# Layer 1's support stage in a hand-written order with four product banks, its first transposes placed at the end of layer 0

## The chip, the cores and the metric

The kernel runs on one core of a Trainium2 chip. The metric is the device time of one execution in microseconds (us), here the median of a few runs. The engines are named as in the profile: PE (TensorE matmul), PEld (its weight loads), DVE (VectorE), ACT (ScalarE), POOL (GpSimd) and SP (SyncE, which here only issues DMAs). SBUF is the on-chip working memory, PSUM the buffer with eight banks into which PE writes.

## The reference

Four graph layers follow each other on x (4096 × 256, float32) with one 0/1 adjacency matrix adj (4096 × 4096). Each layer ends in a layernorm of x plus the layer's result.

```python
# layer 0: attention over the adjacency, 8 heads of 32
x = layernorm(x + L0(x, W, b, a, adj))
# layer 1: the layer of this change
support = x @ weight                      # 4096 x 256
A = jnp.diagonal(adj) + adj               # the diagonal is added to every row
x = layernorm(x + (A @ support + bias))
# layer 2: two steps of top-p attention and of diffusion over adj + I
x = layernorm(x + L2(x, adj, W1, W2, W3, U1, U2, ln_g, ln_b))
# layer 3: mean over neighbours, one product, relu
x = layernorm(x + L3(x, adj, W, b))
```

Since the diagonal is added to every row, A @ support is adj @ support plus one row, diagonal @ support, which is the same for all rows of the result.

## The kernel before

Rows are tiled in NB = 32 blocks of 128. X, the running x, stays in SBUF for all 32 blocks.

**Layer 0** goes through its heads in two halves, and in each through four stretches of eight row blocks. A head accumulates into a PSUM tile `acc` of four banks; two buffers of it take all eight banks. After a head DVE reduces acc (L334) and a chain of short DVE steps follows (L338 to L345). In the second half the two halves of the columns are added to X (L359 on POOL, L360 on POOL or, for the last eight blocks, on DVE), two blocks at a time. Each such pair of blocks goes into the list `later`; its layernorm is done on POOL while a later head runs. Four pairs, the blocks 24 to 31, are left over and handed to layer 1 as `self.later`.

**Layer 1, the support stage** (`layer1`) first prepares two small weight products for layer 2 (`attention_weights`: two transposes L758, two copies L759, matmuls L762, and copies into `wkq` L763 and L764). Their inputs lie in the tile `xT1[1]` until they are used. Then it goes through eight groups of four row blocks. For a group, `transposed` (L99 to L110) makes eight 128 × 128 transposes on PE into two `ps_tp` banks (L108) and ACT copies them (L109) into one of the two tiles `xT1`. In groups 1 to 4 the layernorm of one left-over pair runs: `moments` takes statistics on DVE (L85, L86), POOL works out the inverse deviation (L88, L89), and DVE normalizes (L96). Then each of the four blocks is multiplied by the weight into a `ps_sup` bank (L781), and `split` writes the product in two parts into XD: the rounded value by ACT (L126) and the remainder by DVE (L127). There are two `ps_sup` banks, two `ps_tp` and two `ps_adj`. After the groups, 32 matmuls with the diagonal (L786) give the common row.

**Layer 1, the product.** For each of the 32 row blocks b, four pieces of the adjacency (128 × 8 × 128) are cast from bytes `na` into `adj_piece`, on DVE for even and on ACT for odd pieces (L206, L204). There are eight piece buffers, two blocks' worth. 32 matmuls (L802) multiply them by XD into `ps_adj`. `keep` writes every piece out to `adjs` in DRAM for the later layers, on SP's queue (L161, L165, L168), with the identity added to the block on the diagonal by POOL (L164). The bytes come in by ACT's DMA queue, four loads of 1 MB for eight row blocks (`bytes_of`, L189), in eight buffers. A block ends with three additions to X, a layernorm and a store (L807 to L811).

**What sets the order.** Nothing in this stretch is ordered by hand. A scheduler lists the instructions of every engine by its own estimates, so work of the product (casts, write-outs, ps_adj matmuls) is mixed into the support stage. The order is fixed once compiled, and each engine goes through its list in that order. Inside `tc.manual_schedule(...)` the named engines follow the order of the program text; layers 2 and 3 use it in places already.

Of the kernel before, what the change touches and what calls it, by code (L numbers as in the profile page):

```python
# [9 lines left out]
F32 = mybir.dt.float32  # L10
I32 = mybir.dt.int32
F32R = mybir.dt.float32r
BF16 = mybir.dt.bfloat16
FP8 = mybir.dt.float8e4
# [5 lines left out]
ET = mybir.EngineType  # L20
# [3 lines left out]
P = 128  # L24
# [31 lines left out]
class Net:  # L56
# [135 lines left out]

    def adj_pieces(self, pool, nas, b, G=8):

        nc = self.nc
        at = b * P % self.IT
        if at == 0:
            nas[:] = self.bytes_of(pool, b)
        pieces = []
        for g in range(self.NB // G):  # L200
            a = pool.tile([P, G, P], F32R, name="adj_piece", bufs=2 * (self.NB // G))
            edges = nas[g][:, :, at:at + P].bitcast(FP8)
            if g % 2:
                nc.scalar.mul(a, edges, 2.0 ** 5)  # L204
            else:
                nc.vector.tensor_scalar_mul(a, edges, 2.0 ** 5)  # L206
            pieces.append(a)
        return pieces

# [3 lines left out]
    def layer0(self):  # L215
        nc, tc, NB, D, N = self.nc, self.tc, self.NB, self.D, self.N
# [3 lines left out]
        Q = IT // P  # L220
        keep = self.ctx.enter_context(tc.tile_pool(name="l0k", bufs=1, space=DRAM))
        self.fits = keep.tile([1, 1], I32, name="fits")
        with ExitStack() as ctx:
            pool = ctx.enter_context(tc.tile_pool(name="l0", bufs=1))
# [58 lines left out]
            X, xr = self.X, self.rows(self.x)  # L283
            gp = ctx.enter_context(tc.tile_pool(name="l0gm", bufs=1))
            work = ctx.enter_context(tc.tile_pool(name="l0w", bufs=2))
            psum = ctx.enter_context(tc.tile_pool(name="l0ps", bufs=2, space=PSUM))
# [6 lines left out]
            for half in range(2):  # L293
                for it in range(N // IT):
# [14 lines left out]
                    for hh in range(H // 2):  # L309
# [4 lines left out]
                        acc = psum.tile([P, Q, 256], F32, name="acc")  # L314
                        for g in range(NB // K):
# [8 lines left out]
                            for k in range(K):  # L324
                                jc = g * K + k
                                for q in range(Q):
# [3 lines left out]
                                                     start=(jc == 0 and q % 2 == 0),  # L330
                                                     stop=(jc == NB - 1 and q % 2 == 1))
# [25 lines left out]
                    for q in range(0, Q, 2):  # L357
# [2 lines left out]
                        engine.tensor_add(xs[:, :, D // 2:], xs[:, :, D // 2:], y[:, q:q + 2])  # L360
                        later.append(xs)
            self.later = later

    def choose0(self, fac, zd, gmd, gm0):

        with self.tc.If(self.nc.values_load(self.fits, min_val=0, max_val=1) == 0):  # L366
            self.general0(fac, zd, gmd, gm0)
# [384 lines left out]
    def attention_weights(self, psum):  # L752

        nc, A = self.nc, 64
        aw1, aw3, aw2, w1 = self.attention_parts()
        for c in range(2):
            pt = psum.tile([P, 512], F32, name="ps_sup")
            nc.tensor.transpose(pt[:A, :P], aw1[:, c, :], self.ident)  # L758
            nc.scalar.copy(w1[:, c, :], pt[:A, :P])  # L759
        for c in range(2):  # L760
            pt = psum.tile([P, 512], F32, name="ps_sup")
            nc.tensor.matmul(pt[:, :A], w1[:, c, :], aw2, start=True, stop=True)  # L762
            nc.vector.tensor_copy(self.wkq[:, c, 1, :], pt[:, :A])  # L763
            nc.vector.tensor_copy(self.wkq[:, c, 0, :], aw3[:, c, :])  # L764

    def layer1(self):
        nc, tc, NB, D, X = self.nc, self.tc, self.NB, self.D, self.X
        with self.ctx1 as ctx:
            pool, w1, bias, dg = self.pool1, self.weight1, self.bias1, self.diagr
            work = ctx.enter_context(tc.tile_pool(name="l1w", bufs=2))  # L770
            psum = ctx.enter_context(tc.tile_pool(name="l1ps", bufs=2, space=PSUM))
            XD = self.XD
            self.attention_weights(psum)
            for g in range(NB // 4):
                xT = self.transposed(psum, work, X[:, 4 * g:4 * g + 4, :], "xT", out=self.xT1[g % 2])
                if 1 <= g <= 4:
                    self.layernorm(work, self.later[g - 1], self.later[g - 1])
                for q in range(4):
                    ps = psum.tile([P, 512], F32, name="ps_sup")
                    for c in range(2):  # L780
                        nc.tensor.matmul(ps[:, :D], xT[:, c, q * P:(q + 1) * P], w1[:, c, :],  # L781
                                         start=(c == 0), stop=(c == 1))
                    self.split(XD[:, 4 * g + q], ps[:, :D])
            pd = psum.tile([P, 512], F32, name="ps_sup")
            for jc in range(NB):
                nc.tensor.matmul(pd, dg[:, jc:jc + 1].to_broadcast([P, P]), XD[:, jc].rearrange("p s d -> p (s d)"),  # L786
                                 start=(jc == 0), stop=(jc == NB - 1))
            row = pool.tile([P, D], F32, name="row1")
            nc.vector.tensor_add(row, pd[:, :D], bias)
            nc.vector.tensor_add(row, row, pd[:, D:])  # L790

            nas = []
            ahead = self.adj_pieces(work, nas, 0)
            for b in range(NB):
                ps = psum.tile([P, 512], F32, name="ps_adj")
                now, ahead = ahead, None
                for g, a in enumerate(now):

                    self.keep(work, a, b, g)
                    for k in range(8):  # L800
                        jc = g * 8 + k
                        nc.tensor.matmul(ps, a[:, k, :], XD[:, jc].rearrange("p s d -> p (s d)"),  # L802
                                         start=(jc == 0), stop=(jc == NB - 1))
                if b + 1 < NB:
                    ahead = self.adj_pieces(work, nas, b + 1)
                xb = X[:, b:b + 1, :]
                nc.vector.tensor_add(xb[:, 0], xb[:, 0], ps[:, :D])  # L807
                nc.vector.tensor_add(xb[:, 0], xb[:, 0], ps[:, D:])
                nc.vector.tensor_add(xb[:, 0], xb[:, 0], row)
                self.layernorm(pool, xb, xb)  # L810
                nc.gpsimd.dma_start(self.xd[b, :, 0, :], xb[:, 0])  # L811
# [1158 lines left out]
```

## Time and profile before

| | |
|---|---|
| median of 3 runs | 4007.29 us (4001.58 to 4010.75) |
| the profiled execution | 4011.93 us, of which the span is 4010.2 us |
| PE busy in the span | 3906.8 us (97%) |
| DVE, ACT, POOL busy | 2990.2, 2742.6, 1136.7 us (75%, 68%, 28%) |
| last matmul of layer 0 ends | 1322.3 us |
| support stage, with the diagonal | 1324.2 to 1395.9 us |
| last matmul of layer 1's product starts | 1623.4 us |

Times inside the span count from its start. The profile is of one execution, and a matmul's end in it is modelled: the pitch from one start to the next says more than a busy time. A row of the timeline gives start, time, engine, source line, operation, output and inputs and a count of merged instructions; in brackets stands the idle time of that engine before it and who ended it. A line such as L96 is in a helper and has several callers.

### The profile page before, as it was taken

Reading aid. Unit: us, or ns where it says so; the run is one execution under the profiler, and the core shown is the slowest. Engines: PE = TensorE matmul, PEld = TensorE weight load, DVE = VectorE, ACT = ScalarE, POOL = GpSimd, SP = SyncE. Lnnn points to the kernel's source line nnn. Section 1 sums busy time; section 2 is a strip of 40 time slices with the busy share of each in tenths; the row PEclk is TensorE's granted clock in tenths of the full one; section 3 lists DMA queues with packets and bytes.
Section 4 is the critical chain, followed back from the end, with each engine's and each line's share of the span. In section 5 each row is a group of like instructions: output and inputs, shape, how many; then the busy total and the mean of one; then the engine's idle time right before and its main releaser. Section 6 shows DMA issues by size and latency. Waiting matters only on the chain. (4 is left out here: it accounts for less than half of the span.)

```text
span 4010.2 us, 68765 instructions
## 1 busy us (share of the span) xinstructions
PE 3906.8 (97%) x25081; PEld 3377.3 (84%) x25081; DVE 2990.2 (75%) x6647; ACT 2742.6 (68%) x5119; POOL 1136.7 (28%) x1394
## 2 busy tenths in 40 slices
PE   8899998999999899999999999999999999999899
PEld 7899998999999788678888888865888888888687
DVE  7742228999999444567878788837999999999365
ACT  5532228999999322468888888825888888888132
POOL 1321111111344022411111111114555555555211
PEclk9999999999999999999999999999999999999999
DMA  4765557335222498533333333463333333335541
GB/s 130 228 204 176 176 168 224 90 108 136 69 78 70 170 359 324 154 119 96 100 97 101 95 102 92 137 203 105 108 107 104 108 118 99 107 120 184 186 158 49
DMA packets 317403, 557.36 MB, mean 139 GB/s; under 512 B 72646, under 2 KB 139734, under 8 KB 312950
## 3 DMA queue, kind: packets, MB, share of 16 engines
q1 hardware_dynamic: 242368, 396.99, 31.4%
q0 software_dynamic: 32224, 98.75, 7.5%
q10 hardware_dynamic: 42454, 57.04, 4.3%
q8 instruction: 203, 3.33, 0.3%
q14 instruction: 154, 1.26, 0.1%
HBM read 386.71 MB, written 165.94 MB: 138 GB/s over the span
## 5 line engine op out<-in xcount | busy, mean ns | idle before, releaser
L1359 PE MATMUL ps_a<-X,aT 128*128 128x256 f32 x4096 | 970.4, 379 | 1.3 <-ACT h L1500 1.1
L1359 PEld LDWEIGHTS ps_a<-X,aT 128*128 128x128 f32 x4096 | 774.1, 190 | 127.2 <-issue 3.3
L328 PE MATMUL acc<-gm,gt 128*128 128x198 bf16 x8192 | 702.5, 248 | 14.2 <-DVEq L366 5.6
L328 PEld LDWEIGHTS <-gt 128*128 128x128 fp8e4 x8192 | 700.4, 97 | 16.2 <-issue 11.3
L273 ACT ACTIVATE sg<-lpb,nlc 128x1024 fp8e4<-128x1024 f32 x632 | 664.0, 1135 | 48.5 <-DVE gt L275 33.8
L550 PE MATMUL pz<-src,ar 128*128 128x264 f32 x4096 | 513.5, 288 | 20.6 <-DVE ar L540 18.6
L550 PEld LDWEIGHTS pz<-src,ar 128*128 128x128 f32 x4096 | 510.3, 191 | 23.7 <-DVE ar L540 21.3
L180 PE MATMUL ps_r<-XD,adj_piece 128*128 128x512 f32 x1888 | 528.4, 414 | 1.0 <-DMA adj_piece<-adjs 1.0
L1086 ACT ACTIVATE ja<-e,nc 128x2048 uint8<-128x2048 f32 x240 | 480.9, 2004 | 2.0
L1352 ACT COPY aT<-ps_tp 128x512 f32<-128x512 f32 x512 | 296.4, 579 | 216.7 <-PE ps_tp L1350 214.5
L180 PEld LDWEIGHTS ps_r<-XD,adj_piece 128*128 128x128 f32 x1888 | 332.9, 189 | 70.2 <-issue 12.9
L1151 DVE MAX8 cand<-v 128x8 f32<-128x256 f32 x1024 | 347.1, 411 | 4.4
L1201 DVE SCALAR_TENSOR_TENSOR e<-e,edge 128x512 f32<-128x512 f32 x512 | 347.9, 751 | 2.1
L543 ACT ACTIVATE nb<-ar 128x512 uint8<-128x512 f32 x256 | 147.5, 623 | 268.4 <-DVE ar L540 265.2
L1350 PE MATMUL ps_tp<-ident,e 128*128 128x128 f32 x2048 | 307.7, 273 | 0.0
L1147 DVE SCALAR_TENSOR_TENSOR v<-e,hi 128x2048 f32<-128x2048 f32 x128 | 299.8, 2342 | 2.4
L1350 PEld LDWEIGHTS ps_tp<-ident,e 128*128 128x128 f32 x2048 | 256.5, 141 | 51.4 <-issue 0.5
L267 DVE TENSOR_SCALAR sg<-lpb,nlc 128x1024 fp8e4<-128x1024 f32 x384 | 285.2, 778 | 6.6 <-SPq L366 4.4
L995 ACT ACTIVATE e<-ps_logit 128x1024 f32<-128x1024 f32 x256 | 260.2, 1027 | 26.6 <-PE ps_logit L993 26.4
L993 PE MATMUL ps_logit<-kT,q 128*128 128x512 f32 x1024 | 274.1, 409 | 4.0 <-ACT e L995 1.7
L540 DVE CAST ar<-a 128x1024 fp32r<-128x1024 f32 x128 | 88.9, 695 | 248.1 <-PE pz L550 242.4
L802 PE MATMUL ps_adj<-XD,adj_piece 128*128 128x512 f32 x1024 | 244.9, 398 | 1.2 <-POOL ln_var L88 1.2
(396 smaller groups left out, 5577.5 us busy)
## 6 DMA issues: line engine op xcount, KB each, us to landing
adj_piece<-adjs SPq DMA_DIRECT2D x552, 256.0 KB, 2.9
a<-in_adjt_dram SPq DMA_DIRECT2D x256, 256.0 KB, 3.0
adjs<-adj_piece SPq DMA_DIRECT2D x96, 512.0 KB, 3.4
na<-nad SPq DMA_DIRECT2D x64, 512.0 KB, 4.5
lpb<-lpd POOLq DMA_DIRECT2D x32, 512.0 KB, 4.2
nad<-nb POOLq DMA_DIRECT2D x128, 128.0 KB, 2.8
na<-nad ACTq DMA_DIRECT2D x16, 1024.0 KB, 5.6
gmd<-gb POOLq DMA_DIRECT2D x64, 198.0 KB, 3.9
```

The source lines that it names most:

```text
L180: nc.tensor.matmul(ps, a[:, k, :], rhs(jc).rearrange("p s d -> p (s d)"), start=(jc == 0), stop=(jc == self.NB - 1))
L267: nc.vector.tensor_scalar(sg[:, k, :], lpb, nlc[:, 4 * g + k, h:h + 1], 2.0 ** -5, op0=ALU.is_ge, op1=ALU.mult, saturate=False)
L273: nc.scalar.activation(sg[:, k, :], lpb, AF.Sign, scale=-1.0, bias=nlc[:, 4 * g + k, h:h + 1], saturate=False)
L328: nc.tensor.matmul(acc[:, q, :6 * C1], gt[:, k, q * P:(q + 1) * P], gm0[:, jc, :] if head0 else gm[:, jc, hh, :], start=(jc == 0 and q % 2 ...
L550: nc.tensor.matmul(pz[q][:, t, :W], ar[:, q, k, :], src[:, jc, t, s], start=(jc == 0 and s == 0), stop=(jc == NB - 1 and s == 1))
L1086: nc.scalar.activation(ja, e[:, s * HALF:(s + 1) * HALF], f, bias=nc1, accum_out=fs[:, i + s:i + s + 1])
L1147: nc.vector.scalar_tensor_tensor(v, ec, hi, ec, op0=ALU.is_lt, op1=ALU.mult, accum_out=sb[:, s:s + 1])
L1151: nc.vector.max(cand[:, 8 * j:8 * j + 8], v[:, k * 256:(k + 1) * 256])
L1201: nc.vector.scalar_tensor_tensor(ec, ec, edge[:, j:j + 1], ec, op0=ALU.is_ge, op1=ALU.mult)
L1350: nc.tensor.transpose(pt[:, k * P:(k + 1) * P], e[:, jc * P:(jc + 1) * P], self.ident)
L1352: nc.scalar.copy(aT, pt)
L1359: nc.tensor.matmul(pa[:, :D], aT[:, k * P:(k + 1) * P], X[:, jc, :], start=(jc == 0), stop=(jc == NB - 1))
```

## The change

- The whole support stage stands in a manual schedule for PE, ACT, DVE, POOL and SP.
- `ps_sup` has four banks instead of two, so that the stage's pool takes all eight banks.
- The transposes of group 0 move to the end of layer 0, into a buffer of `acc`; ACT copies them to `xT1[0]`. Those of group g + 1 stand between the second and the third product tile of group g.
- `attention_weights` becomes a generator: its transposes come first, its matmuls and copies after the second product tile.
- The four left-over layernorms normalize on POOL instead of DVE, after the tiles of groups 0 to 3.
- The first four loads of bytes are issued after group 1. The four pieces of block 0 are cast one each after groups 4 to 7. To this end `adj_pieces` is split, and `adj_part` casts a single piece.

```diff
--- before.py
+++ after.py
@@ -192,20 +192,21 @@
 
     def adj_pieces(self, pool, nas, b, G=8):
 
+        if b * P % self.IT == 0:
+            nas[:] = self.bytes_of(pool, b)
+        return [self.adj_part(pool, nas, b, g) for g in range(self.NB // G)]
+
+    def adj_part(self, pool, nas, b, g, G=8):
+
         nc = self.nc
         at = b * P % self.IT
-        if at == 0:
-            nas[:] = self.bytes_of(pool, b)
-        pieces = []
-        for g in range(self.NB // G):
-            a = pool.tile([P, G, P], F32R, name="adj_piece", bufs=2 * (self.NB // G))
-            edges = nas[g][:, :, at:at + P].bitcast(FP8)
-            if g % 2:
-                nc.scalar.mul(a, edges, 2.0 ** 5)
-            else:
-                nc.vector.tensor_scalar_mul(a, edges, 2.0 ** 5)
-            pieces.append(a)
-        return pieces
+        a = pool.tile([P, G, P], F32R, name="adj_piece", bufs=2 * (self.NB // G))
+        edges = nas[g][:, :, at:at + P].bitcast(FP8)
+        if g % 2:
+            nc.scalar.mul(a, edges, 2.0 ** 5)
+        else:
+            nc.vector.tensor_scalar_mul(a, edges, 2.0 ** 5)
+        return a
 
 
 
@@ -360,6 +361,12 @@
                         engine.tensor_add(xs[:, :, D // 2:], xs[:, :, D // 2:], y[:, q:q + 2])
                         later.append(xs)
             self.later = later
+            acc = psum.tile([P, Q, 256], F32, name="acc").rearrange("p q c -> p (q c)")
+            for c in range(2):
+                half = acc[:, c * 512:(c + 1) * 512]
+                for q in range(4):
+                    nc.tensor.transpose(half[:, q * P:(q + 1) * P], X[:, q, c * P:(c + 1) * P], self.ident)
+                nc.scalar.copy(self.xT1[0][:, c, :], half)
 
     def choose0(self, fac, zd, gmd, gm0):
 
@@ -754,11 +761,12 @@
         nc, A = self.nc, 64
         aw1, aw3, aw2, w1 = self.attention_parts()
         for c in range(2):
-            pt = psum.tile([P, 512], F32, name="ps_sup")
+            pt = psum.tile([P, 512], F32, name="ps_sup", bufs=4)
             nc.tensor.transpose(pt[:A, :P], aw1[:, c, :], self.ident)
             nc.scalar.copy(w1[:, c, :], pt[:A, :P])
+        yield
         for c in range(2):
-            pt = psum.tile([P, 512], F32, name="ps_sup")
+            pt = psum.tile([P, 512], F32, name="ps_sup", bufs=4)
             nc.tensor.matmul(pt[:, :A], w1[:, c, :], aw2, start=True, stop=True)
             nc.vector.tensor_copy(self.wkq[:, c, 1, :], pt[:, :A])
             nc.vector.tensor_copy(self.wkq[:, c, 0, :], aw3[:, c, :])
@@ -770,18 +778,31 @@
             work = ctx.enter_context(tc.tile_pool(name="l1w", bufs=2))
             psum = ctx.enter_context(tc.tile_pool(name="l1ps", bufs=2, space=PSUM))
             XD = self.XD
-            self.attention_weights(psum)
-            for g in range(NB // 4):
-                xT = self.transposed(psum, work, X[:, 4 * g:4 * g + 4, :], "xT", out=self.xT1[g % 2])
-                if 1 <= g <= 4:
-                    self.layernorm(work, self.later[g - 1], self.later[g - 1])
-                for q in range(4):
-                    ps = psum.tile([P, 512], F32, name="ps_sup")
-                    for c in range(2):
-                        nc.tensor.matmul(ps[:, :D], xT[:, c, q * P:(q + 1) * P], w1[:, c, :],
-                                         start=(c == 0), stop=(c == 1))
-                    self.split(XD[:, 4 * g + q], ps[:, :D])
-            pd = psum.tile([P, 512], F32, name="ps_sup")
+            nas, ahead = [], []
+            with tc.manual_schedule(engines={ET.PE, ET.Activation, ET.DVE, ET.Pool, ET.SP}):
+                setup = self.attention_weights(psum)
+                next(setup)
+                for g in range(NB // 4):
+                    xT = self.xT1[g % 2]
+                    for q in range(4):
+                        ps = psum.tile([P, 512], F32, name="ps_sup", bufs=4)
+                        for c in range(2):
+                            nc.tensor.matmul(ps[:, :D], xT[:, c, q * P:(q + 1) * P], w1[:, c, :],
+                                             start=(c == 0), stop=(c == 1))
+                        self.split(XD[:, 4 * g + q], ps[:, :D])
+                        if q == 1:
+                            if g == 0:
+                                for _ in setup:
+                                    pass
+                            if g < NB // 4 - 1:
+                                self.transposed(psum, work, X[:, 4 * g + 4:4 * g + 8, :], "xT", out=self.xT1[(g + 1) % 2])
+                    if g < 4:
+                        self.layernorm(work, self.later[g], self.later[g], nc.gpsimd)
+                        if g == 1:
+                            nas[:] = self.bytes_of(work, 0)
+                    else:
+                        ahead.append(self.adj_part(work, nas, 0, g - 4))
+            pd = psum.tile([P, 512], F32, name="ps_sup", bufs=4)
             for jc in range(NB):
                 nc.tensor.matmul(pd, dg[:, jc:jc + 1].to_broadcast([P, P]), XD[:, jc].rearrange("p s d -> p (s d)"),
                                  start=(jc == 0), stop=(jc == NB - 1))
@@ -789,8 +810,6 @@
             nc.vector.tensor_add(row, pd[:, :D], bias)
             nc.vector.tensor_add(row, row, pd[:, D:])
 
-            nas = []
-            ahead = self.adj_pieces(work, nas, 0)
             for b in range(NB):
                 ps = psum.tile([P, 512], F32, name="ps_adj")
                 now, ahead = ahead, None
```

## The prediction

> **What bounds the kernel now.** I read the page first: TensorE (PE) is busy 97% of the span, so a change pays only where PE idles or runs slowly. I compared the compiled instruction order of the two kernels next: apart from line and tile numbers, they differ on every engine only from the end of layer 0's last head to the first blocks of layer 1's product. So I cut that stretch into windows (columns: us, then busy time with instruction count of PE, PEld, DVE, ACT, POOL; granted clock; DMA share; GB/s).
>
> ```profile
> 1322.00:1396.00 74.00, 62.88 (x283) 50.88 (x282) 29.38 (x77) 25.85 (x56) 6.26 (x12) 0.91 0.59 206
> 1322.00:1332.00 10.00, 8.08 (x32) 6.29 (x31) 6.73 (x17) 2.34 (x6) 0.00 (x0) 0.66 0.00 1
> ...
> 1366.00:1373.00 7.00, 6.07 (x16) 4.90 (x17) 1.78 (x4) 2.14 (x6) 0.00 (x0) 0.51 1.02 364
> ...
> 1410.00:1500.00 90.00, 90.00 (x388) 72.11 (x387) 42.98 (x96) 25.43 (x24) 22.74 (x50) 1.00 0.93 361
> ```
>
> From 1322 to 1396 PE idles 74.00 − 62.88 = 11.1 us, and for about 7 us twice it runs at half clock. From 1410 on it never idles at full clock: the product is bound by PE, so whatever the stage before it saves reaches the end of layer 1. Next PE's own timeline:
>
> ```profile
> 1324.22 0.41 PE L758 MATMUL ps_sup<-ident,xT 128*64 128x128 f32 x2 [1.90 <-DVE red L334]
> ...
> 1337.32 1.96 PE L781 MATMUL ps_sup<-w,xT 128*128 128x256 f32 x8 [3.15 <-DVE XD L127]
> ...
> 1346.56 1.89 PE L781 MATMUL ps_sup<-w,xT 128*128 128x256 f32 x8
> 1348.29 1.04 PE L108 MATMUL ps_tp<-ident,X 128*128 128x128 f32 x8
> 1349.08 0.71 PE L802 MATMUL ps_adj<-XD,adj_piece 128*128 128x512 f32 x2
> ...
> 1366.93 2.07 PE L781 MATMUL ps_sup<-w,xT 128*128 128x256 f32 x4 [4.00 <-DVE XD L127]
> ...
> 1388.41 7.67 PE L786 MATMUL ps_sup<-XD,diagr 128*128 128x512 f32 x32
> 1395.92 4.36 PE L802 MATMUL ps_adj<-XD,adj_piece 128*128 128x512 f32 x18
> ```
>
> Who made PE wait 3.15 and 4.00 us is seen on DVE and ACT:
>
> ```profile
> 1336.43 0.41 DVE L96 TENSOR_SCALAR X<-X,ln_mv,ln_rstd 128x256 f32<-128x256 f32 x1 [0.83 <-POOL ln_rstd L89]
> 1336.76 0.75 DVE L127 TENSOR_TENSOR XD<-ps_sup,XD 128x256 fp32r<-128x256 f32 x2
> ...
> 1365.10 1.06 ACT L204 ACTIVATE adj_piece<-na 128x1024 fp32r<-128x1024 fp8e4 x1 [5.51 <-DMA adjs<-adj_piece]
> ...
> 1366.06 0.63 ACT L126 CAST XD<-ps_sup 128x256 fp32r<-128x256 f32 x2
> ```
>
> Both are queueing, not work. The subtractions that free the two ps_sup banks stand behind layernorm steps that wait for POOL; later the copies out of ps_sup stand behind a cast of an adjacency piece for a later block, which waits until its buffer has been written out.
>
> **What the Trainium skill says.** "TensorE: Matmul & The Clock Gate", section "What's actually happening": the clock halves after an idle window of about 3.4 us and returns after a busy one. The trace agrees: 0.50 from 1325 to 1332 after a gap of 1.9 us and thin work, and 0.51 from 1366 to 1373 after the gap of 4.0; each lasts about two such windows. "PSUM — Partial Sum Buffer", section "Engine vs sequencer instructions": ScalarE's, VectorE's and GpSimd's queues are strict FIFO; the fence above shows it. "SBUF — State Buffer", section "Who interferes with whom": a DVE instruction with two SBUF inputs, or in a two-port mode, blocks a GpSimd instruction that reads SBUF; one with at most one SBUF input does not. The trace has both prices for POOL's layernorm step, with DVE nearly full of mask work (X) and elsewhere (h):
>
> ```profile
> L96 POOL TENSOR_SCALAR h<-h,ln_mv,ln_rstd x64: 1239/1244/1248, 2828.0 to 3779.4; 128x256 f32<-128x256 f32 x64
> L96 POOL TENSOR_SCALAR X<-X,ln_mv,ln_rstd x24: 1217/2286/3707, 1074.4 to 1279.7; 128x256 f32<-128x256 f32 x24
> ```
>
> **The change part by part.** First the work that PE cannot avoid before 1395.92, in steady rates: two product tiles take 1348.29 − 1346.56 = 1.73 us, so 32 take 27.7; eight transposes 0.79, so eight groups 6.3; diagonal 7.5; attention weights about 1.0; a ps_adj matmul 0.2335 (blocks of 16 follow each other at 3.74 us), and 48 of them stand before 1395.92: 11.2. Sum 53.7, against 1395.92 − 1322.32 (the last head's end) = 73.6. So 19.9 us are to be had: 11.1 idle, up to 6.8 of half clock (0.34 of 10 us, 0.49 of 7), the rest pacing by two banks (two tiles per 2.06 us around 1381).
>
> *Start.* Eight transposes go into the free acc buffer while DVE reduces the last head; the first half's ACT copy (0.59) stands before the second half's transposes, so with about 0.2 per handover xT1[0] is ready near 1324.8. The weights' transposes wait for that and for the reduction (1324.17): PE starts its first two tiles near 1325.0, against 1327.2 before. Weights and transposes for group 1 follow to 1328.1, tiles 2 and 3 to 1329.8. Group 1's xT overwrites xT1[1], which holds the attention weights, so its ACT copies wait for the four wkq copies on DVE. Those stand behind the end of the last head, the four additions L360 (1.43), and two subtractions: near 1329.65. Two copies later group 1 can run; its tiles count from about 1330.4.
>
> *Groups 1 to 7.* Four banks allow 4 × 0.865 = 3.46 us from one use of a bank to its next; the round trip of a bank (matmul 0.87, ACT 0.37, DVE 0.42, handovers) was 2.06. So PE sets the pace: 3.46 + 0.79 = 4.25 per group. ACT needs 4 × 0.37 + 2 × 0.54 = 2.6, DVE 4 × 0.42 plus about 1.1 for the statistics = 2.8: both are hidden. Seven groups, less the last one's transposes, plus six ps_adj matmuls that stay inside (1.4): 29.8 − 0.8 + 1.4, ending near 1360.8.
>
> *Moved: na loads.* Four issues of 1 MB stand together on ACT after group 1. A similar four elsewhere, on SP:
>
> ```profile
> 3791.72 2.13 SPq L1844 DMA_DIRECT2D X<-nad  x4
> ```
>
> 2.1 us on ACT delays group 2's copies and, through its second xT, PE by about 0.5; bounds 0 and 2. The first load starts at about 1337 instead of 1331.25, and with 5.6 us to landing is there by 1343; its cast on DVE comes after group 4, near 1348.5. The second four are single issues, 0.33 each, hidden in ACT's slack. SP's write-outs start at 1349 instead of 1341, its own-block part behind POOL's last layernorm. Nothing reads these bytes in layer 1; they only free the eight piece buffers, first needed again after 1369.
>
> *Moved: layernorms to POOL.* Eight DVE steps of 0.41 vanish; POOL gets per group 0.23 + 0.72 + 2 × 1.24 plus gaps = 3.6 us. The DVE work beside it reads PSUM and at most one SBUF operand, so I take 1.24; the dear end is 2.3 to 3.7. At 3.6 they end by about 1350; the last rows are transposed near 1354.
>
> *Sum.* 1360.8 + 0.5 = 1361.3; diagonal 7.5: 1368.8. The 42 ps_adj matmuls no longer done by then: 9.8. That is 1378.6 against 1395.9: 17.3 us less. If the clock still halves at the start (gaps of about 1.5 us remain there), the first tiles to 1332 cost 3 us more. I take 16.3, one third of that. The profiled execution is 4011.93, of which the span is 4010.2: it would come to 3995.6. The median of the runs is 4007.29, 4.6 below it: 3991.0.
>
> **The rivals.**
> *DMA becomes the bound.* By the windows some 88 MB move between 1330 and 1624. In the shorter stage they would have from 1337 to 1607, 327 GB/s. Against it: from 1400 to 1600 the same mix already moved 343 GB/s on average, with PE never idle. For it: the share touches 1.03. If writes hold PE up at the end, most of the gain goes: 4004, within 0.2%.
> *Partial.* POOL's four layernorms run at the 7.8 us of layer 0's tail (four of them from 1251.3 to 1282.3). Started at 1333.3, they end at 1364.5 where 1354 is needed: 10.5 lost, 4001; a halved clock and a longer issue on ACT alone give 3995.
> *Slower.* The same place at its worst: the longest of those four took 1263.96 to 1275.71, 11.7 us. Four such end at 1380.1. The last transposes, and DVE's aggregates that need a free ln_mv buffer, wait 26 us: 17 saved, 26 lost, 4016. It decides from (1371.3 − 1333.3)/4 = 9.5 us each. Against it speaks what DVE runs here.
> *The change doesn't do what it says.* The compiled order excludes this: four banks, and only six ps_adj matmuls in the stage.
>
> **How the numbers follow.** About 0.2% (8 us) is what a measurement of this kernel can tell from no change; three runs of before spread over 9. Main case (13 to 18 saved, 3989 to 3995): 0.71. Partial (3996 to 4003): 0.14. DMA bound or otherwise nothing: 0.08. Slower: 0.07. Faster by over 0.2% means below 3999.3: the main case and more than half of the partial one, 0.79; same 0.14; slower 0.07. The range runs from 3984 (all 19.9 saved and a low draw of the runs) to 4003.
>
> **What would show it.** Right: the last ps_adj matmul starts near 1606 to 1607 instead of 1623.4; the diagonal near 1361; PE pitch 4.25 per group without gaps over 1 us after group 1; POOL's L96 at 1.2 to 1.4 us; clock 1.0 after about 1332; no cast of a piece in front of a copy out of ps_sup while it waits for a write-out. Wrong: L96 over 5 us a pair, DVE's ln_mv waiting for POOL, ACT held at the na issues for over 3 us, or PE idle inside the product after 1369.

## The result, and the profile after

| | before | after |
|---|---|---|
| median | 4006.89 us (6 runs, 4001.58 to 4012.31) | 3992.61 us (6 runs, 3989.53 to 3996.99) |
| profiled execution, its span | 4011.93, 4010.2 us | 3993.55, 3991.9 us |
| layer 0's last head ends on PE | 1322.32 | 1320.87 |
| layer 2's first matmul (ps_logit) starts | 1624.88 | 1605.61 |
| S, the difference of the last two | 302.56 | 284.74 |

The ratio of the times is 0.9963, with a 95% interval of 0.9953 to 0.9974: faster, by some 15 us. S is the yardstick of all that follows. It holds layer 1 whole and the DVE chain behind layer 0's last head, so it leaves out what layers 0, 2 and 3 do differently from one execution to the next: here layer 0 ended 1.45 us earlier, and the rest after layer 1 took 2386.3 instead of 2385.3. S fell by 17.8 us.

The windows of the kernel after; the columns are us, then busy time with instruction count of PE, PEld, DVE, ACT and POOL, then granted clock, DMA share, GB/s:

```profile
1322.00:1396.00 74.00, 73.32 (x357) 61.86 (x358) 37.12 (x96) 31.54 (x61) 20.93 (x31) 1.00 0.71 279
1322.00:1332.00 10.00, 9.32 (x54) 7.99 (x55) 7.83 (x24) 5.14 (x13) 0.68 (x2) 1.00 0.01 2
1366.00:1373.00 7.00, 7.00 (x32) 5.66 (x31) 2.14 (x4) 1.06 (x1) 0.47 (x1) 1.00 0.72 277
1396.00:1600.00 204.00, 204.00 (x876) 164.35 (x875) 97.15 (x218) 55.91 (x53) 51.03 (x109) 1.00 0.85 331
```

PE now idles 0.68 of the 74 us (and as much just ahead of them), not 11.1, and the clock is 1.00 in both stretches where it was 0.66 and 0.51. After 1396 PE never idles, as before. PE's timeline after (start, time, then the row as described above):

```profile
1321.98 0.66 PE L368 MATMUL acc<-ident,X 128*128 128x128 f32 x4 [0.68 <-ACT xT L369]
...
1323.32 0.41 PE L765 MATMUL ps_sup<-ident,xT 128*64 128x128 f32 x2 [0.68 <-ACT xT L369]
1323.56 1.89 PE L790 MATMUL ps_sup<-w,xT 128*128 128x256 f32 x8
...
1326.90 3.62 PE L790 MATMUL ps_sup<-w,xT 128*128 128x256 f32 x16
1330.35 1.04 PE L108 MATMUL ps_tp<-ident,X 128*128 128x128 f32 x8
1331.22 3.62 PE L790 MATMUL ps_sup<-w,xT 128*128 128x256 f32 x16
...
1359.26 7.76 PE L807 MATMUL ps_sup<-XD,diagr 128*128 128x512 f32 x32
```

Two handovers of 0.68 us at the start are all that is left of the waits; then one group follows another every 1331.22 − 1326.90 = 4.32 us. The four loads on ACT's queue and POOL's first two layernorms, from their timelines:

```profile
1333.31 2.01 ACTq L189 DMA_DIRECT2D na<-nad  x4
1335.36 0.65 ACT L126 CAST XD<-ps_sup 128x256 fp32r<-128x256 f32 x2 [1.84 <-PE ps_tp L108]
```

```profile
1332.37 2.43 POOL L96 TENSOR_SCALAR X<-X,ln_mv,ln_rstd 128x256 f32<-128x256 f32 x2
1335.15 0.23 POOL L88 TENSOR_SCALAR ln_var<-ln_mv 128x2 f32<-128x2 f32 x1 [0.34 <-DVE ln_mv L86]
1335.46 0.72 POOL L89 TENSOR_TENSOR ln_rstd<-ln_var,power 128x2 f32<-128x2 f32 x1
1336.29 2.44 POOL L96 TENSOR_SCALAR X<-X,ln_mv,ln_rstd 128x256 f32<-128x256 f32 x2
```

ACT makes no copy for 1.84 us beside the four issues (2.01 us), and PE's row of 16 matmuls across that time shows no gap. POOL takes 1.22 us per step of L96 and waits for DVE, not DVE for it.

### The profile page after: what moved, and what is told of

The parts are those of the page before. It is cut to its first block, busy times and chain, and to the rows that moved or that the text cites. A ratio compares the mean times of both kernels' runs of the same rounds, so it can differ in the third digit from the quotient of the medians.

```text
span 3991.9 us, 68776 instructions
## 1 busy us (share of the span) xinstructions
PE 3896.7 (98%) x25081; PEld 3372.9 (84%) x25081; DVE 2991.4 (75%) x6639; ACT 2745.8 (69%) x5119; POOL 1155.2 (29%) x1402
## 5 line engine op out<-in xcount | busy, mean ns | idle before, releaser
L329 PEld LDWEIGHTS <-gt 128*128 128x128 fp8e4 x8192 | 700.4, 97 | 14.7 <-issue 9.1
L821 PE MATMUL ps_adj<-XD,adj_piece 128*128 128x512 f32 x1024 | 239.8, 396 | 0.0
## 6 DMA issues: line engine op xcount, KB each, us to landing
na<-nad ACTq DMA_DIRECT2D x16, 1024.0 KB, 11.1
```

The costliest lines, as they stand in the source:

```text
L329: nc.tensor.matmul(acc[:, q, :6 * C1], gt[:, k, q * P:(q + 1) * P], gm0[:, jc, :] if head0 else gm[:, jc, hh, :], start=(jc == 0 and q % 2 ...
```

## The experiments

Twelve kernels ran. The question was which part of the change earns the 17.8 us: theory A says the order, theory B the four banks. S of each is from its own one profiled execution, the ratio is of medians, to runs of before taken beside it.

| kernel | S | ratio (95% interval) |
|---|---|---|
| before | 302.6 | |
| before, layernorm on POOL alone | 299.1 | 1.0002 (0.9993 to 1.0011) |
| after, POOL steps added, 7.9 us a layernorm | 296.2 | 0.9987 (0.9978 to 0.9997) |
| after, order alone | 295.0 | 0.9995 (0.9986 to 1.0003) |
| after without the manual order | 294.3 | 0.9988 (0.9979 to 0.9996) |
| before, four banks alone | 292.7 | 0.9984 (0.9977 to 0.9991) |
| after with two banks | 291.0 | 0.9981 (0.9972 to 0.9991) |
| after, three banks, layernorm on DVE | 289.4 | 0.9967 (0.9953 to 0.9982) |
| after, late transposes | 287.0 | 0.9957 (0.9940 to 0.9973) |
| after, early casts | 286.5 | 0.9960 (0.9946 to 0.9974) |
| after, POOL steps added, 5.5 us a layernorm | 285.8 | 0.9963 (0.9949 to 0.9978) |
| after, layernorm on DVE | 285.6 | 0.9965 (0.9951 to 0.9979) |
| after | 284.7 | 0.9963 (0.9953 to 0.9974) |
| after, both halves transposed first | 284.7 | 0.9963 (0.9948 to 0.9977) |

An interval is ±3 to ±7 us wide, so differences of one or two us among the last six rows are read in S and its trace alone. What a row saves against before's 302.6 most likely holds some 2.3 us of a half clock at the start of before's one profiled execution (see the section on the prediction); differences between two other rows do not hold it.

**Banks without the order.** The kernel before, with one edit at four places:

```diff
-            pt = psum.tile([P, 512], F32, name="ps_sup")
+            pt = psum.tile([P, 512], F32, name="ps_sup", bufs=4)
```

> The kernel before with four ps_sup banks and nothing else; the scheduler orders all. Theory A (order): the waits for POOL in front of subtractions and the casts that wait for write-outs remain, as do the idle start and the half clock: S 296 to 301. Theory B (banks): the buffers ride out the waits: S 286 to 291.

S was 292.7, between the two ranges: banks alone save 9.9. No cast in the stage waits for a write-out any more; in before one cost PE 4.0 us. That is not shown to be the buffer riding out a wait: with four banks the scheduler also made another list, with 29 instead of 48 ps_adj matmuls and five instead of six ACT casts (L204) ahead of the diagonal, and in this list no cast has to wait. What is left is a pile of layernorm steps, here on DVE and then on PE:

```profile
1328.64 0.73 DVE L96 TENSOR_SCALAR X<-X,ln_mv,ln_rstd 128x256 f32<-128x256 f32 x2 [1.09 <-POOL ln_rstd L89]
...
1330.68 0.41 DVE L96 TENSOR_SCALAR X<-X,ln_mv,ln_rstd 128x256 f32<-128x256 f32 x1 [0.83 <-POOL ln_rstd L89]
1331.00 0.75 DVE L127 TENSOR_TENSOR XD<-ps_sup,XD 128x256 fp32r<-128x256 f32 x2
```

```profile
1331.47 1.99 PE L781 MATMUL ps_sup<-w,xT 128*128 128x256 f32 x8 [1.40 <-DVE XD L127]
...
1337.73 5.18 PE L781 MATMUL ps_sup<-w,xT 128*128 128x256 f32 x16 [0.97 <-DVE XD L127]
```

The scheduler puts several pairs' steps together, ahead of the subtractions L127; their waits for POOL add up to more than four banks hold. The row of 5.18 for 16 matmuls (elsewhere 3.62) is a half clock after these gaps.

**The order with two banks.** The same edit taken back in the kernel after (`bufs=4` removed at the four places).

> The changed kernel with two ps_sup banks instead of four. Measure: S, from the end of layer 0's last matmul to layer 2's first (302.6 us before, 284.7 after the change). Theory A, the order pays (no subtraction or copy out of ps_sup stands behind a wait any more): two banks cost only their round trip, 0.3 to 0.7 us per group, S 287 to 290. Theory B, the four banks pay: S 296 or more. Time after plus 2 to 5 us under A, plus 11 or more under B.

S was 291.0, just above A's range: the other parts without the banks save 11.6, and with the other parts in place the banks are worth 6.3. Groups follow at 4.65 instead of 4.33 us (the first ones at 5.08 and 4.75), and at the start PE waits behind L360's additions, which stand as L361 here; a half clock follows:

```profile
1324.77 0.43 PE L770 MATMUL ps_sup<-xT 64*128 64x64 f32 x2 [1.24 <-DVE XD L127]
...
1326.06 5.63 PE L790 MATMUL ps_sup<-w,xT 128*128 128x256 f32 x16
```

That half clock is about 1.7 of the 6.3: the next row of 16 matmuls took 3.94.

**The order alone.** The kernel after with two banks, the layernorm on DVE, and group 0's transposes in layer 1:

```diff
-                        self.layernorm(work, self.later[g], self.later[g], nc.gpsimd)
+                        self.layernorm(work, self.later[g], self.later[g])
...
                 next(setup)
+                self.transposed(psum, work, X[:, 0:4, :], "xT", out=self.xT1[0])
```

> The fixed order alone: two ps_sup banks, layernorm steps on DVE, group 0's transposes inside layer 1. Theory A: S 288 to 292 (4 us for the banks and the layernorms, 2 to 3 for the start, perhaps with a half clock). Theory B: S 297 or more.

S was 295.0, again between: 7.6 saved, too little for the median to tell (0.9986 to 1.0003). No cast stands in the way, but each layernorm on DVE does, once per group:

```profile
1335.78 4.05 PE L785 MATMUL ps_sup<-w,xT 128*128 128x256 f32 x16 [1.29 <-DVE XD L127]
...
1341.97 4.04 PE L785 MATMUL ps_sup<-w,xT 128*128 128x256 f32 x16 [1.27 <-DVE XD L127]
```

**Everything but the order.** The manual schedule removed, so that the scheduler orders the changed program:

```diff
-            with tc.manual_schedule(engines={ET.PE, ET.Activation, ET.DVE, ET.Pool, ET.SP}):
+            with ExitStack():
```

> The changed kernel without the manual schedule: four banks, early transposes, layernorm steps on POOL, the scheduler's own order. Theory A: S 290 to 297, since casts and statistics again stand in front of the copies out of ps_sup. Theory B: S 285 to 287.

S was 294.3, in A's range: with four banks and all other parts, the order is worth 9.6. What its pieces are worth each (the transposes between the tiles, the late loads of bytes, the spread statistics) was not run, except for the place of the casts, below. Two long holds make the loss. DVE's and ACT's timelines of this kernel:

```profile
1330.45 0.18 DVE L86 BATCH_NORM_AGGREGATE ln_mv<-ln_stats 128x2 f32<-128x6 f32 x1 [2.84 <-POOL X L96]
```

```profile
1345.18 1.06 ACT L206 ACTIVATE adj_piece<-na 128x1024 fp32r<-128x1024 fp8e4 x1 [3.85 <-DMA na<-nad]
```

And what they do to PE:

```profile
1331.72 5.41 PE L790 MATMUL ps_sup<-w,xT 128*128 128x256 f32 x16 [2.37 <-DVE XD L127]
...
1349.19 3.42 PE L790 MATMUL ps_sup<-w,xT 128*128 128x256 f32 x8 [3.28 <-ACT xT L109]
```

The first is a wait that the layernorm on POOL brought in: statistics of several pairs stand together, and a later pair's needs an ln_mv buffer that POOL's L96 still reads. The second is a cast put in front of the copies of xT before its bytes had come. PE lost 5.65 us in the two, and twice a half clock behind them.

**The layernorm on POOL alone**, in the kernel before.

```diff
-                    self.layernorm(work, self.later[g - 1], self.later[g - 1])
+                    self.layernorm(work, self.later[g - 1], self.later[g - 1], nc.gpsimd)
```

> The kernel before with one part of the change alone: the four left-over layernorms normalize on POOL. In before, DVE stood at L96 waiting for POOL's rstd with the subtractions that free the two banks behind it. Theory A (two banks and the scheduler's order still hold PE up, by casts that wait for a write-out and by pacing): about a third of the idle time goes, S 297 to 301. Theory B (it was the layernorm on DVE that made the stage slow): S 288 to 294.

S was 299.1, as theory A has it, and no difference in the median. DVE no longer waits for rstd, but for the buffer, and longer:

```profile
1329.56 0.18 DVE L86 BATCH_NORM_AGGREGATE ln_mv<-ln_stats 128x2 f32<-128x6 f32 x1 [2.84 <-POOL X L96]
```

```profile
1330.91 3.75 PE L781 MATMUL ps_sup<-w,xT 128*128 128x256 f32 x8 [4.69 <-DVE XD L127]
```

The cast behind a write-out is still there too (ACT idle 4.61 for adjs, PE 3.11). One wait was exchanged for another.

**The layernorm on DVE, with four and with three banks.** The first line of the order-alone diff, and for three banks `bufs=3` at the four places.

> The changed kernel with the four left-over layernorms' normalizing steps back on DVE, in the fixed order. With two banks and the same steps on DVE (the order alone) PE stood 1.3 to 1.5 us in each of four groups. Theory A, four banks ride out a DVE that is held for about 2 us (1.0 for POOL's result, 0.8 of its own steps): S 285 to 286.5, no gap over 0.5 us. Rival: moving them to POOL is a part of the gain of its own: gaps stay, S 289 to 291.

> The changed kernel with the layernorm on DVE (285.6 with four banks) and three product banks instead of four. Each bank adds one tile's 0.865 us to the delay that PE rides out. With two banks the same layernorm made gaps of 1.3 to 1.5 us in four groups. Theory: with three about 0.4 us remains of each, S 286.5 to 288.5. Rival (three are as good as four, since the round trip of a bank fits in three): S 285 to 286.2.

With four banks S was 285.6, as theory A expected. With three it was 289.4, a little above the range. The gap that the layernorm leaves on PE in its second group, in the kernel with three banks:

```profile
1337.25 1.03 PE L790 MATMUL ps_sup<-w,xT 128*128 128x256 f32 x4
1339.02 2.86 PE L790 MATMUL ps_sup<-w,xT 128*128 128x256 f32 x12 [0.75 <-DVE XD L127]
...
1342.59 1.03 PE L790 MATMUL ps_sup<-w,xT 128*128 128x256 f32 x4
```

The pitch of such a group is 6.19 us with two banks (1335.78 to 1341.97 in the fence above), 5.34 with three (1337.25 to 1342.59), and with four 4.33 to 4.53, once 4.95. So the third bank is worth 0.85, close to one tile's 0.865, as expected, and the fourth another 0.8 to 1.0 (once 0.4), which brings the groups to PE's own pace or near it. The 0.4 that I expected to remain was too small because I took one bank off the visible gap of 1.27, when two banks also slow the tiles beside it (a row of 16 took 4.04 instead of 3.62).

**POOL made dearer.** Extra steps after each left-over layernorm that leave the values as they are; first four per pair with plain numbers:

```diff
                         self.layernorm(work, self.later[g], self.later[g], nc.gpsimd)
+                        for q in range(2):
+                            for i in range(2):
+                                xq = self.later[g][:, q, :]
+                                nc.gpsimd.tensor_scalar(xq, xq, 1.0, 0.0, op0=ALU.mult, op1=ALU.add)
```

> The changed kernel with four more steps of 128 x 256 on POOL per left-over layernorm (multiply by 1, add 0, in place), so that one takes about 8.5 us instead of 3.9. It prices the slower rival of the prediction. If POOL's chain is on the path from about 5.2 us on, the last transposes wait to about 1366 instead of 1352: S 297 to 303. If POOL is off the path: S within 1 of 284.7.

The steps cost 0.44 each, not the 1.2 that I had reckoned with, so a layernorm took some 5.5 us and S stayed at 285.8: the test was too weak to decide. It showed the edge, however: PE waited 0.53 for POOL in the last group's transposes. The second try had seven steps with both numbers read per partition:

```diff
+                        ones = work.tile([P, 2], F32, name="ones")
+                        nc.vector.memset(ones[:, 0:1], 1.0)
+                        nc.vector.memset(ones[:, 1:2], 0.0)
+                        for q in range(2):
+                            for i in range(4 if q else 3):
+                                xq = self.later[g][:, q, :]
+                                nc.gpsimd.tensor_scalar(xq, xq, ones[:, 0:1], ones[:, 1:2], op0=ALU.mult, op1=ALU.add)
```

> The changed kernel with seven more steps on POOL in each of the four left-over layernorms, times one plus zero with both numbers read per partition as in L96 itself, so that the values stay the same. S is the time from the end of layer 0's last matmul to the start of layer 2's first (before 302.6, changed kernel 284.7). If a step costs what L96 costs here (1.22), a layernorm takes 3.6 + 8.5 = some 12 us on POOL and four of them end near 48 us after the first starts; the second pair is then 11 us late and the last one 30 us late for its transposes. Theory (the slower rival of the prediction): S 309 to 317, at or above before. Rival (POOL is not on the path, or a part of the wait is covered by product matmuls moved up): below 300. If the step costs 0.44 as with plain numbers, S stays below 292.

Again a step cost less than expected, 0.63; POOL's and PE's timelines:

```profile
1337.85 2.44 POOL L96 TENSOR_SCALAR X<-X,ln_mv,ln_rstd 128x256 f32<-128x256 f32 x2
1340.26 4.39 POOL L807 TENSOR_SCALAR X<-X,ones 128x256 f32<-128x256 f32 x7
1344.62 0.23 POOL L88 TENSOR_SCALAR ln_var<-ln_mv 128x2 f32<-128x2 f32 x1
```

```profile
1345.27 1.97 PE L790 MATMUL ps_sup<-w,xT 128*128 128x256 f32 x8 [1.58 <-DVE XD L127]
...
1352.73 0.33 PE L108 MATMUL ps_tp<-ident,X 128*128 128x128 f32 x1 [0.82 <-POOL X L807]
1358.12 0.47 PE L108 MATMUL ps_tp<-ident,X 128*128 128x128 f32 x1 [5.06 <-POOL X L807]
1360.62 1.33 PE L108 MATMUL ps_tp<-ident,X 128*128 128x128 f32 x5 [2.03 <-POOL X L807]
```

A layernorm takes 7.9 us (1336.71 to 1344.62), and S was 296.2, 11.5 more than after and inside "below 300". The place is the one named in the prediction: the last group's transposes wait 0.82 + 5.06 + 2.03 = 7.9 us. The 1.58 ahead of them is most likely the experiment's own: the two `memset` of `ones` wait on DVE for the end of POOL's steps two layernorms back, in front of a subtraction. The rest is a half clock (3.30 us for the next 8 matmuls, elsewhere 1.89).

**Group 0's transposes in layer 1** (the early ones removed, `transposed` called after `next(setup)` as above).

> The changed kernel with group 0's transposes inside layer 1, after those of the attention weights. Theory A: PE starts its first tile about 2 us later and the start is worth that alone, S 286 to 288; if the idle start halves the clock as it did before, 289 to 291. Rival, the start is hidden behind DVE's chain and the four copies to wkq: S within 1 of 284.7.

S was 287.0. PE's timeline has both the wait and a half clock:

```profile
1321.47 0.41 PE L759 MATMUL ps_sup<-ident,xT 128*64 128x128 f32 x2 [1.90 <-DVE red L335]
1321.92 1.94 PE L108 MATMUL ps_tp<-ident,X 128*128 128x128 f32 x8
```

The early transposes are worth 2.3 us between these two executions. Some 1.7 of it is the half clock: the eight transposes took 1.94 (1.06 in the order-alone kernel, after the same gap) and the eight product matmuls behind them 2.72 instead of 1.89. How much they are worth when the clock stays whole was not shown, and the medians tell nothing (0.9957 here, 0.9963 after). With a half clock I had expected 289 to 291, too much: it ended within 16 matmuls.

**Casts earlier.** The four casts of block 0 after groups 1 to 4 instead of 4 to 7.

```diff
-                    else:
-                        ahead.append(self.adj_part(work, nas, 0, g - 4))
+                    if 1 <= g <= 4:
+                        ahead.append(self.adj_part(work, nas, 0, g - 1))
```

> The changed kernel with the casts of block 0's pieces after groups 1 to 4 instead of 4 to 7, while the byte loads are still issued after group 1. DVE's cast then stands in the fixed order in front of the next subtractions and waits for its load. Theory A, place in the queue decides: DVE held for 3 to 5 us, PE idle for 2 to 4, S 287 to 290, more if the clock halves. Rival, four banks hide it: S 284 to 286.

S was 286.5, between the ranges. The first cast holds DVE until its bytes come:

```profile
1335.22 0.69 DVE L208 TENSOR_SCALAR adj_piece<-na 128x1024 fp32r<-128x1024 fp8e4 x1 [3.13 <-DMA na<-nad]
1335.83 1.41 DVE L127 TENSOR_TENSOR XD<-ps_sup,XD 128x256 fp32r<-128x256 f32 x4
```

```profile
1332.58 1.89 PE L790 MATMUL ps_sup<-w,xT 128*128 128x256 f32 x8
1336.02 2.10 PE L821 MATMUL ps_adj<-XD,adj_piece 128*128 128x512 f32 x8 [1.54 <-issue]
```

PE lost 1.54 of the 3.13. Its wait stands at product matmuls for the adjacency (L821), which need the cast piece, the only one so far, and start 0.11 us after its cast ends, so most likely PE waited for the piece itself. The banks would hardly have let it go on sooner: four products stood in them, and the four subtractions that free them begin at 1335.83. So about half of this hold was ridden out.

**Both halves transposed before either is copied**, an attempt to win the last 1.36 us of waiting (the two gaps of 0.68).

```diff
                 for q in range(4):
                     nc.tensor.transpose(half[:, q * P:(q + 1) * P], X[:, q, c * P:(c + 1) * P], self.ident)
-                nc.scalar.copy(self.xT1[0][:, c, :], half)
+            for c in range(2):
+                nc.scalar.copy(self.xT1[0][:, c, :], acc[:, c * 512:(c + 1) * 512])
```

> The changed kernel with all eight early transposes in front of the two copies, instead of transposes, copy, transposes, copy. The two waits of 0.68 us of PE at the start are all that PE still idles in the stage. Theory A: the DVE chain after the last head (reduction, additions, wkq copies) sets when group 1 can run, so an earlier start ends in a wait there: S within 0.5 of 284.7. Theory B: the handover between PE and ACT sets it, S 283.3 to 284.1.

S was 284.7, no gain, as theory A has it in size. PE waited 1.23 us once instead of 0.68 twice, since both copies (1.07 us) now come after all transposes, and the first full row of 16 matmuls took 3.93 instead of 3.62. That DVE's chain is what sets this was not shown. No version ran that is better than the kernel after by more than the runs can tell.

## Why the prediction was right

- **What bounds it** held: from 1400 to 1595 PE was busy without a gap in before, after and all twelve experiments, and S fell by 17.8 where the sum said 17.3.
- **The start.** First tile 2.7 us after the last head's end, as worked out (1325.0 − 1322.32; measured 1323.56 − 1320.87). Group 1's tiles began 7.8 after it where 8.1 was taken: the wkq copies were done at 6.7, not 7.3.
- **The half clock at the start**, of which the prediction took a third, did not come; that is the 1 us between 17.3 and 16.3. The two gaps of 0.68 were shorter than the 1.5 that I had in mind. Both numbers count the half clock at before's own start as a part of before (see the last point).
- **The pitch** was 4.33, not 4.25: eight transposes between two product tiles take 0.87 (1330.35 to 1331.22), and I had priced them from a place where a product matmul follows, 0.79. This costs some 0.5 over the groups, and the four issues on ACT, priced at 0.5, cost PE nothing. The diagonal began 38.4 after the last head's end; the sum has 39.0.
- **The moves.** Six product matmuls inside, the first cast on DVE at 1346.89, POOL's layernorms at 1.22 to 1.4 per step and done by 1347.8: these as named. The loads of bytes went out earlier, 12.4 us after the last head's end (1333.31) where 14.7 was taken. No copy stood behind a cast that waited for a write-out.
- **The rivals.** DMA moved 331 GB/s between 1396 and 1600 at a share of 0.85 and held PE up nowhere. The partial case's price was nearly right: at 7.8 us a layernorm it lost 10.5, and the dear kernel at 7.9 lost 11.5, of which 1.6 most likely not POOL's. The slower case's price was not run. From the dear kernel 302.6 − 296.2 + 1.6 = 8.0 us are left until S is that of before; at four layernorms each 2.0 dearer this puts the turn near 9.9 us (9.5 was said), by extrapolation, and near 9.3 without the 2.3 us of before's half clock. Its second wait, DVE's aggregates behind ln_mv, is real but needs no dear POOL: it cost PE 4.69 and 2.37 us in the two kernels in which the scheduler had put several pairs' statistics together.
- **The total** was closer than its parts. In the profiled executions 18.4 us went, in the medians 14.3 (the ratio's interval: 10 to 19). I had taken 16.3 for both, by carrying over the 4.6 us that before's profiled execution lay above its median; after's lies 0.9 above. That 16.3 lies between the two is in part luck. Over the thirteen kernels the medians' ratio gives on average 2.4 us less than S (from 1.7 more to 5.5 less). The most likely reason is the start of before's profiled execution, where PE had a granted clock of 0.53 and 0.50 (1325 to 1329 and 1329 to 1332). The kernel with the layernorm on POOL alone runs the same instructions there after the same gap of 1.90, at 1.00. First PE and DVE of before, then of that kernel:

```profile
1327.21 3.78 PE L781 MATMUL ps_sup<-w,xT 128*128 128x256 f32 x8
1331.78 0.74 DVE L85 BATCH_NORM_STATS2 ln_stats<-X 128x6 f32<-128x256 f32 x2
```

```profile
1321.63 1.99 PE L781 MATMUL ps_sup<-w,xT 128*128 128x256 f32 x8 [0.24 <-ACT xT L109]
1324.40 0.74 DVE L85 BATCH_NORM_STATS2 ln_stats<-X 128x6 f32<-128x256 f32 x2
```

From the last head's end to the first statistics (L85) before takes 1331.78 − 1322.32 = 9.46 us, the other 1324.40 − 1317.26 = 7.14: 2.3 us. The kernel with four banks alone takes 7.14 as well. So some 2.3 of the 17.8 are most likely a half clock that before does not have in every execution; since no other execution of before was profiled, this is not shown.

What the prediction did not say is which part pays. No part alone does it all: in S, banks save 9.9, order 7.6, the layernorm on POOL 3.5, each with the 2.3 of before's start in it; in the medians 6.4, 2.0 and −0.8, each ±3 to ±4, so that of these three only the banks' saving is clear of nothing. With four banks in place, the order is worth 9.6, and in one execution each the early transposes 2.3 (1.7 of it half clock), the casts' late place 1.8, and the layernorm on POOL 0.9. The four banks rode out about 1.6 us of a hold of 3.13 in the kernel with early casts; the order sees to it that no longer ones occur, by spreading the pairs' statistics and putting each cast after its bytes.

## What to carry to other kernels

An in-order engine that frees PSUM banks can be late by about one tile's matmul time (here 0.865 us) per spare bank before PE notices, so count banks against the longest hold in that queue, and look at which instruction in front of the freeing one waits, and for whom. Moving a step to an idle engine can exchange the wait for one on its double buffer, unless the producers are spread out as well. An order written by hand and a deeper buffer cover different holds; try them together before judging either.

## What the runs showed of the hardware

- POOL's price of the same instruction form, in place on 128 × 256 float32, differs by a factor of 2.8 with its operations and scalars: subtract and multiply with both numbers per partition, from two tiles, 1.22 us (L96), multiply and add with both per partition, from one tile, 0.63, multiply and add with plain numbers 0.44. Whether the operations or the place of the numbers make the first step of this was not separated. That L96 written as a multiply and an add would take half was not tried.
- The same gap of 1.90 us at the start left the clock whole in one kernel and halved it in another. The order-alone kernel shows:

```profile
1317.22 0.41 PE L759 MATMUL ps_sup<-ident,xT 128*64 128x128 f32 x2 [1.90 <-DVE red L335]
1317.65 1.06 PE L108 MATMUL ps_tp<-ident,X 128*128 128x128 f32 x8
```

The kernel with late transposes has the same two rows with 1.94 us for the eight transposes; before had the half clock after this gap, the kernels with the layernorm on POOL alone and with four banks alone did not. The Trainium skill, "TensorE: Matmul & The Clock Gate", section "What's actually happening", says that the window is free-running, so that a transition depends on where in it the work falls. These rows fit that, though each is one execution and no run here shows the window itself. The prediction read the half clock behind before's gap of 1.9 us as agreeing with an idle window of about 3.4 us. PE's gaps ahead of half clocks were shorter than that in several kernels (1.24 us with two banks, 1.90 here), with little work around them (in before PE was busy for 1.08 of the 3 us from 1322 to 1325); how much work keeps the clock whole was not measured.
